# GRU, attention and AUGRU on one core: zeros on TensorE ahead of the first input, another PSUM ring for the item part, results placed by a 0/1 matrix, and another order of the branches

## The chip, the cores and the metric

The kernel runs on one core of one Trainium2 chip. The metric is the device time of one launch in microseconds. The engines are called PE (TensorE matmul; PEld is its weight load), DVE (VectorE), ACT (ScalarE), POOL (GpSimd) and SP (SyncE, which here only issues DMAs). [...]

## The reference

B is 1024 rows, T is 100 steps, every vector has 128 elements. A GRU runs over each row's history; its states are the keys. Each key is scored against the row's item by a small network, the scores are masked and go through a softmax over the steps, and pooled is the weighted sum of the keys. The first 100 elements of pooled are then taken as one attention weight per step for a second recurrence (AUGRU) over the keys. The state at the row's own last step goes with four other features into a three-layer network of sigmoids, which gives one number per row.

```python
def gru_step(h, x_t):
    gi = x_t @ gru_Wih.T + gru_bih
    gh = h @ gru_Whh.T + gru_bhh
    ...
    r = jax.nn.sigmoid(i_r + h_r)
    z = jax.nn.sigmoid(i_z + h_z)
    n = jnp.tanh(i_n + r * h_n)
    h_new = (1.0 - z) * n + z * h
...
feat = jnp.concatenate([keys, q, keys - q, q * keys], axis=-1)
score = _mlp(feat, [(att_W0, att_b0), (att_W1, att_b1), (att_W2, att_b2)], jax.nn.relu)
...
pooled = jnp.einsum('bt,btd->bd', attn, keys)
att_seq = pooled.T[:T]
...
# augru_step, with gates r, u and h_hat like a GRU's
u = a_t[:, None] * u
h_new = (1.0 - u) * h + u * h_hat
...
comb = jnp.concatenate([user_embedding, item_embedding, hist_sum, item_embedding * hist_sum, attention_feature], axis=1)
scores = _mlp(comb, [(ph_W0, ph_b0), (ph_W1, ph_b1), (ph_W2, ph_b2)], jax.nn.sigmoid)
```

## The kernel before, in words

**Tiling.** Vectors lie on the 128 partitions, rows of the batch along the free axis, in two halves of 512 (`HB`, `NH`). All products are fp32[...]. A gate of the GRU is one PSUM bank of 128x512, filled in four strips of 32 partitions (L509)[...]. In the profile's shapes 128*32 stands for the weight tile and 128x512 for the moving operand.

**GRU stage (`gru_phase`).** `Half.gru` (from about L490) does one step of one half: gate r (ACT sigmoid, L521), the recurrent part of gate n (ph), its input part (pi), gate z (pz); then DVE and ACT form u (L529, at t=0 L538), pi+u (L539), tanh (L540), the sigmoid of z (L541), h-n, times z, plus n (L544 to L546), kq = h times item (L548), and `keep` copies the new state to SBUF on ACT (hn, L555). At t=0 there is no recurrent part. PSUM has two rings here: `ps`, six banks with the tag "g" for the gates, and `pa`, two banks with the tag "a", which the attention network uses. `attend(t)` (L673) packs the three layers of the scoring network for steps t, t-1 and t-2 into the tiles pm of ring "a", and `take` (L707 f, L712 mv) reads them. `item_part` multiplies the item by its part of the scoring weights (pq, L245), also in ring "a", and ACT copies the result with the bias to q0 (q, L248). PE does it once, after gru(1) of both halves and just before attend(0). The order on every engine is written out by hand (`manual_schedule`). A tile of a ring can be written again only when its last reader is done.

**Start.** SP issues the loads in this order: wih, the first half of x at t=0 (L191), bih, bhh, the second half (L195), whh, item, then the further x tiles. DVE forms brz, the summed biases of r and z (L201). POOL clears hist (L202) and then the weight tiles that are filled block by block. ACT loads its function table (L205).

**Join.** The rows are sorted by length for the AUGRU, so that a step need only do the rows that are still alive. How many these are at each step depends on the data, so there are three copies of `augru_phase` with different widths, and a number computed on the chip (over_d) chooses: copy 0 if the count of steps over its widths is below 1, copy 1 if it is below 2, else copy 2. The test is a compare-and-branch on every engine at L1281. In the run profiled here copy 0 is taken. Code of the copies lies in the order in which it is written. Copy 0 begins with row gathers by POOL (`load_rows`, L173 and L174: an optional pacing copy and an indirect DMA), PE transposes of the first keys (L1055, copied by ACT, L1056), gates of the first step (`first_step`, L996, L998), ACT's stores of pooled to DRAM (pooled_d), gathers of the sorted attention weights out of it (att_r, L144), and PE products that spread a weight row over the partitions (L1011: first, spare). L1022 multiplies such a row by gate u. L1033 to L1037 transpose the weights and store them as att_d, from where SP loads each step's row (L1042).

**AUGRU stage.** Each step has three gates r, u, h (PE L1073 for the key's part, L1077 for the state's; ACT L1085, L1097, L1098; DVE L1101 to L1114). POOL gathers key rows for later steps in between, at places that `spread` computes. Groups of 128 rows that have come to their end go through `predict(g)`: gather of their features (part, L1148 by `rows_of`), two products (L1163, L1168), sigmoids (L1190), L1196, L1201, L1204, and y (ACT, L1207), one result on each of 128 partitions. `rows_of` then scatters y to the output by POOL's indirect DMA, since sorting has permuted the rows (idx_p holds the places). Groups 1 to 7 are jobs spread over the steps; group 0, the longest rows, is `final`, with last=True, after the last step.

**End.** The program's last line (L1350) holds each engine's closing waits, a drain and a barrier of all engines.

Of the kernel before, what the change touches and what calls it, by code (L numbers as in the profile page):

```python
# [9 lines left out]
F32 = mybir.dt.float32  # L10
# [4 lines left out]
ALU = mybir.AluOpType  # L15
# [4 lines left out]
P = 128  # L20
B = 1024
# [51 lines left out]
FREE_BANK, EARLY_BANKS, LATE_BANKS = 6, (2, 5, 6, 0), (3, 4, 1)  # L73

PR = P // NH


@with_exitstack
def kernel(ctx: ExitStack, tc: tile.TileContext, a: dict, out: bass.AP):
# [38 lines left out]
    pooled_d = dram.tile([B, P], F32, name="pooled_d")  # L118
    rlen_d = dram.tile([NG, P], F32, name="rlen_d")
    part_d = dram.tile([B, M0], F32, name="part_d")  # L120

    def load(name, shape, src=None, dt=F32):
        t = const.tile(shape, dt, name=name)
# [58 lines left out]
    def all_of(steps):  # L182
        for _ in steps:
            pass

    def gru_phase(pools):
# [1 line left out]
        nc.sync.dma_start(out=wih, in_=a["wih"])  # L188
        xp = pools.enter_context(tc.tile_pool(name="xp", bufs=8))
        x_first = xp.tile([P, HB], F32, name="x")  # L190
        nc.sync.dma_start(out=x_first, in_=a["hist_x"][0][:, :HB])  # L191
        bih = load("bih", [P, 3])
        bhh = load("bhh", [P, 3])
        x_second = xp.tile([P, HB], F32, name="x")
        nc.sync.dma_start(out=x_second, in_=a["hist_x"][0][:, HB:])  # L195
        whh = load("whh", [P, 3, P])
        nc.sync.dma_start(out=item, in_=a["item"])
        pre = pools.enter_context(tc.tile_pool(name="pre", bufs=1))

        brz = const.tile([P, 2], F32, name="brz")  # L200
        nc.vector.tensor_add(brz, bih[:, 0:2], bhh[:, 0:2])  # L201
        nc.gpsimd.memset(hist, 0.0)  # L202

        table = pre.tile([P, 1], F32, name="table")
# [18 lines left out]
        ps = pools.enter_context(tc.tile_pool(name="ps", bufs=6, space=PSUM))  # L223
        pa = pools.enter_context(tc.tile_pool(name="pa", bufs=2, space=PSUM))

        def attention_weights():
            w0 = load("w0", [P, 4, A0])
            for i in range(NH):
                for f, s in F0[i]:
                    nc.vector.tensor_add(wk[i][:, f], w0[:, 0, s], w0[:, 2, s])  # L230
                    nc.vector.tensor_copy(wkq[i][:, f], w0[:, 3, s])
                    nc.vector.tensor_sub(wq[i][:, f], w0[:, 1, s], w0[:, 2, s])
                    for f1, s1 in F1[i]:
                        nc.sync.dma_start(out=w12[i][f, f1], in_=a["w1"][s, s1])
                    nc.sync.dma_start(out=bm[i][f, :], in_=a["b0"][s, :])
                sc = slice(SC[i], SC[i] + 1)
                for f1, s1 in F1[i]:
                    nc.sync.dma_start(out=w12[i][f1, sc], in_=a["w2"][s1, :])
                    nc.sync.dma_start(out=bm[i][f1, :], in_=a["b1"][s1, :])
                nc.sync.dma_start(out=bm[i][sc, :], in_=a["b2"].partition_broadcast(1))  # L240

        def item_part():
            for i in range(NH):
                pq = pa.tile([P, HB], F32, tag="a", name="pq")
                nc.tensor.matmul(  # L245
                    pq, lhsT=wq[i], rhs=item[:, ts(i, HB)], start=True, stop=True
                )
                nc.scalar.activation(q0[:, ts(i, HB)], pq, AF.Identity, bias=bm[i])  # L248

        def load_later():  # L250
# [2 lines left out]
            once = dict(tag="once")  # L253
            mask_ti = mid.tile([T, B], I32, name="mask_ti", **once)
            nc.sync.dma_start(out=mask_ti, in_=a["mask_ti"])
            yield

            mask_tb = mid.tile([T, B], BF16, name="mask_tb", **once)
# [201 lines left out]
        class Half:  # L460
# [37 lines left out]
            def gru(self, t, after_gate, after_sum):  # L498

                x = self.x[t]  # L500
                h = self.h[t - 1] if t else hist[:, self.cols]
                hn = hp.tile([P, HB], F32, tag="h", name="hn")
                self.h[t] = hn

                def gate(g, parts):
                    p = ps.tile([P, HB], F32, tag="g", name=f"ps{g}")
                    for j, (w, v) in enumerate(parts):
                        for q in range(P // R):
                            nc.tensor.matmul(  # L509
                                p[ts(q, R), :],  # L510
                                lhsT=w[:, g, ts(q, R)],
                                rhs=v,
                                start=(j == 0),
                                stop=(j == len(parts) - 1),
                            )
# [24 lines left out]
                nc.scalar.activation(pi, pi, AF.Tanh, bias=bih[:, 2:3])  # L540
                nc.scalar.activation(pz, pz, AF.Sigmoid, bias=brz[:, 1:2])  # L541
                after_sum()
                d = wp.tile([P, HB], F32, tag="d", name="d")
                nc.vector.tensor_sub(d, h, pi)  # L544
                nc.vector.tensor_mul(d, pz, d)  # L545
                nc.vector.tensor_add(pi, pi, d)  # L546
                kq = wp.tile([P, HB], F32, name="kq", bufs=2 * NH)
                nc.vector.tensor_mul(kq, pi, item[:, self.cols])  # L548
                self.first[t] = hn, kq
                self.copy = hn, pi  # L550
# [407 lines left out]
    def augru_phase(pools, widths, alive):  # L958
# [41 lines left out]
            return gates  # L1000

        def gather_weights(i):
            r = wp.tile([P, GH, P], F32, name="att_r", bufs=2)
            for g in range(GH):
                gather(r[:, g, :], pooled_d, g, i)
            return r
# [23 lines left out]
        def store_weights(i, p):  # L1030

            for g in range(GH):
                nc.tensor.transpose(p[:, ts(g, P)], sorted_rows[i][:, g, :], ident)  # L1033
            rows_t = wp.tile([P, HB], F32, name="att_t", bufs=2)
            nc.vector.tensor_copy(rows_t, p)
            nc.sync.dma_start(out=att_d[i], in_=rows_t[:T, :])
            load_att(2, i)  # L1037
# [98 lines left out]
        def predict(g, last=False):  # L1136
# [10 lines left out]
            def rows_of(out_ap, in_ap, o, i):  # L1147
                nc.gpsimd.indirect_dma_start(  # L1148
                    out=out_ap,
                    out_offset=o and bass.IndirectOffsetOnAxis(ap=idx_p[:, g : g + 1], axis=0),  # L1150
                    in_=in_ap,
                    in_offset=i and bass.IndirectOffsetOnAxis(ap=idx_p[:, g : g + 1], axis=0),
                )
# [51 lines left out]
            yield  # L1205
            y = sp.tile([P, 1], F32, name="y")
            nc.scalar.activation(y, p2, AF.Sigmoid, bias=later["c2"])  # L1207
            rows_of(out.rearrange("(b o) -> b o", o=1), y, True, None)

        def gathers(q):  # L1210
            for i in range(NH):
# [32 lines left out]
        for t in range(1, T):  # L1244
            if t + 1 in FIRST[2:-1]:
                all_of(ahead)
                ahead, due = gathers(FIRST.index(t + 1) + 1), spread(FIRST.index(t + 1) + 1)
            for i in range(NH):
                half_step(t, i)
                for _ in range(due.pop(0) if due else 0):  # L1250
                    next(ahead, None)

                for n, job in enumerate(list(jobs)):
                    job[0] += 1
                    if n == 0 and job[0] > 2 * G and next(job[1], job) is job:
                        jobs.remove(job)
            left = alive[t + 1] if t + 1 < T else 0
            for g in range(1, HB // PR):
                if left <= g * PR < alive[t]:
                    jobs.append([0, predict(g)])  # L1260
                    if left:
                        next(jobs[-1][1])
            if t == T - G:
                final = predict(0, last=True)
                next(final)
        open_state(T - 1, 1)
        next(final)
        last_state(1)
        for _, job in jobs:
            all_of(job)  # L1270
        all_of(final)

    with ExitStack() as pools, tc.manual_schedule():
# [2 lines left out]
    def augru(n):  # L1276
        with ExitStack() as pools, tc.manual_schedule():
            augru_phase(pools, WIDTHS[n], ALIVE[n])

    over = nc.values_load(over_d, min_val=0, max_val=len(LINES))  # L1280
    with tc.If(over < 1) as fits:  # L1281
        augru(0)
    with fits.Else():
        with tc.If(over < 2) as fits:
            augru(1)
        with fits.Else():
            augru(2)


# [64 lines left out]
```

## Time and profile before

| | us |
|---|---|
| median of 3 runs | 2048.63 |
| the three runs | 2044.19, 2048.96, 2048.63 |
| the profiled execution | 2046.78 |
| its span | 2045.0 |
| PE busy | 1994.6 (98%) |
| DVE busy | 1682.1 (82%) |
| POOL busy | 1260.7 (62%) |
| ACT busy | 944.1 (46%) |

The span is the part of the profiled execution that the profile's page covers, 1.8 us less than its time. A line of groups or of the timeline names the source line, the engine, the operation, what it writes and reads (out<-in), the shapes, and the number of instructions; brackets at the end give the idle time of the engine before it and what ended that. Shown as "busy" are only instructions that compute or move; a q behind an engine's name (POOLq) marks its queue of control and DMA-issuing instructions. The AUGRU begins at about 1403 us on PE; the GRU is all that stands ahead of it.

### The profile page before, as it was taken

What the parts mean: (1) busy time and instruction counts of PE and PEld (TensorE: products, weight loads), DVE (VectorE), ACT (ScalarE), POOL (GpSimd) and SP (SyncE); (2) the same over time, 40 slices, a digit from 0 to 9 for tenths busy, and PEclk for the clock granted to TensorE, in tenths of its full rate; (3) what the DMA queues carried; (4) which work ended last, traced back from release to release, by engine and by line L of the source; (5) the groups of instructions that cost most, each with busy time, mean ns of one, the idle gap of its engine ahead of it and who ended that gap; (6) DMA issues with size and microseconds to landing.
All of it is one profiled execution on the core that took longest, in us unless ns stands there. A gap on an engine that the chain in (4) does not pass through costs nothing.

```text
span 2045.0 us, 41241 instructions
## 1 busy us (share of the span) xinstructions
PE 1994.6 (98%) x15452; PEld 1176.7 (58%) x15452; DVE 1682.1 (82%) x3066; ACT 944.1 (46%) x1708; POOL 1260.7 (62%) x1291
## 2 busy tenths in 40 slices
PE   8999999999999999999999999997699999999997
PEld 3655555555555555555555555544344556679997
DVE  6888989888879887878888888996477777878886
ACT  4444444544544454544454444443244444445554
POOL 0233939579796959595969687997543344443431
PEclk9999999999999999999999999999899999999999
DMA  4553333332234334333433232333332333333322
GB/s 118 101 115 97 98 105 113 98 108 86 89 104 114 118 105 119 113 113 97 141 111 97 91 101 69 96 105 108 122 102 91 91 106 103 95 94 86 95 70 36
DMA packets 241645, 205.66 MB, mean 101 GB/s; under 512 B 59271, under 2 KB 204395, under 8 KB 241435
## 3 DMA queue, kind: packets, MB, share of 16 engines
q1 hardware_dynamic: 227498, 170.43, 29.4%
q0 software_dynamic: 12352, 32.31, 5.6%
q8 instruction: 123, 2.02, 0.4%
q14 instruction: 88, 0.71, 0.1%
q10 hardware_dynamic: 1584, 0.20, 0.1%
HBM read 146.82 MB, written 54.40 MB: 98 GB/s over the span
## 4 chain that ended last, share of the span: by engine, by line
PE 92%; DVE 3%; DMA 2%; issue 1%; ACT 1%; another core or an unknown queue 1%; POOL 0%; SPq 0%; DVEq 0%; ACTq 0%; POOLq 0%
PE ps L509 48%; PE pm L673 16%; PE ph L1077 5%; PE pr L1077 5%; PE pu L1077 4%; PE pu L1073 4%; PE ph L1073 4%; PE pr L1073 4%; DMA rows<-keys_d,idx_k 1%; DVE ps L539 0%; DVE u L529 0%; DVE ps L546 0%; DVE d L545 0%; DVE d L544 0%
## 5 line engine op out<-in xcount | busy, mean ns | idle before, releaser
L509 PE MATMUL ps<-x,wih 128*32 128x512 f32 x4800 | 657.2, 594 | 4.4 <-DMA x<-in_hist_x 4.4
L509 PE MATMUL ps<-hn,whh 128*32 128x512 f32 x4752 | 650.1, 592 | 0.6 <-ACT hn L555 0.6
L509 PEld LDWEIGHTS ps<-x,wih 128*32 128x32 f32 x4800 | 281.7, 110 | 241.7 <-issue 220.4
L509 PEld LDWEIGHTS ps<-hn,whh 128*32 128x32 f32 x4752 | 279.6, 110 | 234.2 <-issue 212.0
L494 POOL TENSOR_TENSOR xm<-x,m 128x512 f32<-128x512 f32 x200 | 234.9, 1174 | 146.0 <-DMA m<-mask_d 145.7
L521 ACT ACTIVATE r<-ps,brz 128x512 f32<-128x512 f32 x200 | 137.7, 688 | 394.9 <-PE ps L509 394.7
L495 POOL TENSOR_TENSOR hist<-hist,xm 128x512 f32<-128x512 f32 x200 | 258.7, 1294 | 15.7
L174 POOL DMA_INDIRECT rows<-keys_d,idx_k x220 | 213.2, 969 | 86.2 <-POOL rows L173 48.5
L610 POOL TENSOR_TENSOR pooled<-pooled,kw 128x512 f32<-128x512 f32 x191 | 245.9, 1287 | 15.0
L609 POOL TENSOR_TENSOR kw<-kt,e 128x512 f32<-128x512 f32 x191 | 206.0, 1078 | 70.6 <-DVE e L782 70.6
L673 PE MATMUL pm<-hn,wk 128*32 128x512 f32 x1200 | 237.7, 592 | 5.0 <-ACT hn L555 2.5
L673 PE MATMUL pm<-kq,wkq 128*32 128x512 f32 x1200 | 237.5, 592 | 0.0
L540 ACT ACTIVATE ps<-ps,bih 128x512 f32<-128x512 f32 x200 | 132.4, 662 | 223.9 <-DVE ps L539 223.9
L1085 ACT ACTIVATE c<-ph,bh 128x96 f32<-128x96 f32 (+41 forms) x198 | 96.5, 488 | 295.9 <-PE ph L1077 240.5
L529 DVE SCALAR_TENSOR_TENSOR u<-ps,bhh,r 128x512 f32<-128x512 f32 x198 | 147.5, 745 | 73.1 <-PE ps L509 69.0
L673 PE MATMUL pm<-mv,w 128*32 128x512 f32 (+1 forms) x808 | 197.6, 592 | 0.5 <-ACT mv L712 0.4
L173 POOL COPY rows<-rest 128x1 f32<-128x1 f32 x188 | 35.3, 188 | 217.5 <-DVE rest L1114 213.5
L544 DVE TENSOR_TENSOR d<-hn,ps 128x512 f32<-128x512 f32 x198 | 136.1, 687 | 35.6 <-ACT ps L540 35.2
L1101 DVE TENSOR_TENSOR pu<-pu,c 128x96 f32<-128x96 f32 (+41 forms) x197 | 88.3, 448 | 87.9 <-ACT c L1085 79.8
L545 DVE TENSOR_TENSOR d<-ps,d 128x512 f32<-128x512 f32 x200 | 138.4, 692 | 25.6 <-ACT ps L541 10.9
L555 ACT COPY hn<-ps 128x512 f32<-128x512 f32 x200 | 116.6, 583 | 92.3 <-DVE kq L548 92.3
L539 DVE TENSOR_TENSOR ps<-ps,u 128x512 f32<-128x512 f32 x200 | 140.0, 700 | 21.5 <-PE ps L509 0.5
(181 smaller groups left out, 3235.3 us busy)
## 6 DMA issues: line engine op xcount, KB each, us to landing
x<-in_hist_x SPq DMA_DIRECT2D x212, 256.0 KB
keys_d<-kt SPq DMA_DIRECT2D x48, 1024.0 KB
m<-mask_d SPq DMA_DIRECT2D x200, 128.0 KB
rows<-keys_d,idx_k POOLq DMA_INDIRECT x220
s_b<-mv SPq DMA_DIRECT2D x200, 8.0 KB
keys_d<-kt SPq DMA_DIRECT2D x32, 64.0 KB
at<-att_d SPq DMA_DIRECT2D x34, 48.0 KB
mask_i<-in_mask SPq DMA_DIRECT2D x8, 200.0 KB
```

The lines of the kernel that those rows point to most:

```text
L174: nc.gpsimd.indirect_dma_start(out=r[:, at, :], out_offset=None, in_=keys_d[q], in_offset=bass.IndirectOffsetOnAxis(ap=idx_k[:, k, i : i + ...
L494: nc.gpsimd.tensor_mul(d, x, m)
L495: nc.gpsimd.tensor_add(acc, acc, d)
L509: nc.tensor.matmul(p[ts(q, R), :], lhsT=w[:, g, ts(q, R)], rhs=v, start=(j == 0), stop=(j == len(parts) - 1),)
L529: nc.vector.scalar_tensor_tensor(out=u, in0=ph, scalar=bhh[:, 2:3], in1=r, op0=ALU.add, op1=ALU.mult,)
L539: nc.vector.tensor_add(pi, pi, u)
L545: nc.vector.tensor_mul(d, pz, d)
L609: eng.tensor_mul(d, k, w)
L610: eng.tensor_add(acc, acc, d)
L673: nc.tensor.matmul(p[i][s, :], lhsT=w[:, s], rhs=v, start=start, stop=stop)
L1073: nc.tensor.matmul(p, lhsT=m[:, 1, :], rhs=k, start=True, stop=False)
L1077: nc.tensor.matmul(p, lhsT=m[:, 0, :], rhs=v, start=False, stop=True)
```

## The change

1. **Start.** ACT issues the loads of x_first and x_second, ahead of its table load; SP keeps the others. A tile idle (128x512) of the ring "kq" is cleared by DVE, and PE multiplies it by itself into two tiles pd of ring "a": eight products of 128*32 by 128x512 whose result nobody reads. brz is formed by DVE behind that memset.
2. **Item part.** pq comes from the gates' ring "g" instead of ring "a".
3. **Results.** Groups 1 to 7 scatter y to early_d, a DRAM tensor that SP clears in the GRU stage. Halfway through the AUGRU (t=50) POOL makes two tiles places (iota, then a comparison with the place of each row of group 0): places[p, c] is 1 where c is row p's place. Behind the last job SP loads all of early_d as all_y, 4 rows of 256, each spread over 32 partitions. For group 0, PE multiplies y, spread over 32 columns, by the four quarters of places into one bank (po), DVE adds all_y, and SP stores the 4x256 results to out. The remaining jobs are run before open_state instead of behind last_state.
4. **Branches.** The test is turned round: copies 1 and 2 stand ahead in the code, copy 0 last.

The diff, without three hunks that only give an old tile its own name as its tag (att_r, att_t, kq):

```diff
@@ -73,6 +73,8 @@
 FREE_BANK, EARLY_BANKS, LATE_BANKS = 6, (2, 5, 6, 0), (3, 4, 1)
 
 PR = P // NH
+BQ = B // (P // R)
+HALF_TIME = T // 2
 
 
 @with_exitstack
@@ -118,6 +120,7 @@
     pooled_d = dram.tile([B, P], F32, name="pooled_d")
     rlen_d = dram.tile([NG, P], F32, name="rlen_d")
     part_d = dram.tile([B, M0], F32, name="part_d")
+    early_d = dram.tile([B, 1], F32, name="early_d")
 
     def load(name, shape, src=None, dt=F32):
         t = const.tile(shape, dt, name=name)
@@ -188,17 +191,16 @@
         nc.sync.dma_start(out=wih, in_=a["wih"])
         xp = pools.enter_context(tc.tile_pool(name="xp", bufs=8))
         x_first = xp.tile([P, HB], F32, name="x")
-        nc.sync.dma_start(out=x_first, in_=a["hist_x"][0][:, :HB])
+        nc.scalar.dma_start(out=x_first, in_=a["hist_x"][0][:, :HB])
         bih = load("bih", [P, 3])
         bhh = load("bhh", [P, 3])
         x_second = xp.tile([P, HB], F32, name="x")
-        nc.sync.dma_start(out=x_second, in_=a["hist_x"][0][:, HB:])
+        nc.scalar.dma_start(out=x_second, in_=a["hist_x"][0][:, HB:])
         whh = load("whh", [P, 3, P])
         nc.sync.dma_start(out=item, in_=a["item"])
         pre = pools.enter_context(tc.tile_pool(name="pre", bufs=1))
 
         brz = const.tile([P, 2], F32, name="brz")
-        nc.vector.tensor_add(brz, bih[:, 0:2], bhh[:, 0:2])
         nc.gpsimd.memset(hist, 0.0)
 
         table = pre.tile([P, 1], F32, name="table")
@@ -222,6 +224,16 @@
         kp = pools.enter_context(tc.tile_pool(name="kp", bufs=3 * NH))
         ps = pools.enter_context(tc.tile_pool(name="ps", bufs=6, space=PSUM))
         pa = pools.enter_context(tc.tile_pool(name="pa", bufs=2, space=PSUM))
+
+        idle = wp.tile([P, HB], F32, tag="kq", name="idle", bufs=2 * NH)
+        nc.vector.memset(idle, 0.0)
+        for _ in range(2):
+            p = pa.tile([P, HB], F32, tag="a", name="pd")
+            for q in range(P // R):
+                nc.tensor.matmul(
+                    p[ts(q, R), :], lhsT=idle[:, ts(q, R)], rhs=idle, start=True, stop=True
+                )
+        nc.vector.tensor_add(brz, bih[:, 0:2], bhh[:, 0:2])
 
         def attention_weights():
             w0 = load("w0", [P, 4, A0])
@@ -241,7 +253,7 @@
 
         def item_part():
             for i in range(NH):
-                pq = pa.tile([P, HB], F32, tag="a", name="pq")
+                pq = ps.tile([P, HB], F32, tag="g", name="pq")
                 nc.tensor.matmul(
                     pq, lhsT=wq[i], rhs=item[:, ts(i, HB)], start=True, stop=True
                 )
@@ -253,6 +265,9 @@
             once = dict(tag="once")
             mask_ti = mid.tile([T, B], I32, name="mask_ti", **once)
             nc.sync.dma_start(out=mask_ti, in_=a["mask_ti"])
+            nc.sync.dma_start(
+                out=early_d.rearrange("(p c) o -> p (c o)", p=P), in_=hist[:, : B // P]
+            )
             yield
 
             mask_tb = mid.tile([T, B], BF16, name="mask_tb", **once)
@@ -1205,7 +1220,49 @@
             yield
             y = sp.tile([P, 1], F32, name="y")
             nc.scalar.activation(y, p2, AF.Sigmoid, bias=later["c2"])
-            rows_of(out.rearrange("(b o) -> b o", o=1), y, True, None)
+            if not last:
+                rows_of(early_d, y, True, None)
+                return
+            p = of_pool("po")[:, :BQ]
+            for q in range(P // R):
+                nc.tensor.matmul(
+                    p[ts(q, R), :],
+                    lhsT=y.to_broadcast([P, R]),
+                    rhs=later["places"][q // 2][:, ts(q % 2, BQ)],
+                    start=True,
+                    stop=True,
+                )
+            all_y = later["all_y"]
+            nc.vector.tensor_add(all_y, p, all_y)
+            nc.sync.dma_start(
+                out=out.rearrange("(q c) -> q c", c=BQ),
+                in_=all_y.rearrange("(q r) c -> q r c", r=R)[:, 0, :],
+            )
+
+        def last_places():
+            own = sp.tile([P, 1], F32, name="own3", bufs=1)
+            nc.gpsimd.tensor_copy(own, idx_p[:, 0:1])
+            later["places"] = []
+            for i in range(NH):
+                row = wp.tile([P, HB], F32, tag="att_r", name="places", bufs=2)
+                nc.gpsimd.iota(
+                    row,
+                    pattern=[[1, HB]],
+                    base=i * HB,
+                    channel_multiplier=0,
+                    allow_small_or_imprecise_dtypes=True,
+                )
+                nc.gpsimd.tensor_scalar(row, row, own, None, ALU.is_equal)
+                later["places"].append(row)
+
+        def earlier_results():
+            later["all_y"] = wp.tile([P, BQ], F32, tag="att_t", name="all_y", bufs=2)
+            nc.sync.dma_start(
+                out=later["all_y"],
+                in_=early_d.rearrange("(q c) o -> q (o c)", c=BQ)
+                .unsqueeze(1)
+                .to_broadcast([P // R, R, BQ]),
+            )
 
         def gathers(q):
             for i in range(NH):
@@ -1263,11 +1320,14 @@
             if t == T - G:
                 final = predict(0, last=True)
                 next(final)
+            if t == HALF_TIME:
+                last_places()
+        for _, job in jobs:
+            all_of(job)
+        earlier_results()
         open_state(T - 1, 1)
         next(final)
         last_state(1)
-        for _, job in jobs:
-            all_of(job)
         all_of(final)
 
     with ExitStack() as pools, tc.manual_schedule():
@@ -1278,13 +1338,13 @@
             augru_phase(pools, WIDTHS[n], ALIVE[n])
 
     over = nc.values_load(over_d, min_val=0, max_val=len(LINES))
-    with tc.If(over < 1) as fits:
-        augru(0)
-    with fits.Else():
+    with tc.If(over > 0) as many:
         with tc.If(over < 2) as fits:
             augru(1)
         with fits.Else():
             augru(2)
+    with many.Else():
+        augru(0)
 
 
 # ---- launch: one core; the host only transposes and reshapes ----
```

More of the change, by code (lines that the diff above doesn't have):

```diff
@@ L546, in gru @@
                 nc.vector.tensor_add(pi, pi, d)
-                kq = wp.tile([P, HB], F32, name="kq", bufs=2 * NH)
+                kq = wp.tile([P, HB], F32, tag="kq", name="kq", bufs=2 * NH)
                 nc.vector.tensor_mul(kq, pi, item[:, self.cols])
@@ L1002, in gather_weights @@
         def gather_weights(i):
-            r = wp.tile([P, GH, P], F32, name="att_r", bufs=2)
+            r = wp.tile([P, GH, P], F32, tag="att_r", name="att_r", bufs=2)
             for g in range(GH):
@@ L1033, in store_weights @@
                 nc.tensor.transpose(p[:, ts(g, P)], sorted_rows[i][:, g, :], ident)
-            rows_t = wp.tile([P, HB], F32, name="att_t", bufs=2)
+            rows_t = wp.tile([P, HB], F32, tag="att_t", name="att_t", bufs=2)
             nc.vector.tensor_copy(rows_t, p)
```

## Prediction

> **What bounds the kernel now.** I read the table of stretches first, then the timeline of the first 34 us, the waits of the stretch where the two halves of the program meet, and last the chain of waits and the end of each engine. Columns of the stretches: start and end, length, then the busy time of PE, PEld, DVE, ACT, POOL, the TensorE clock, the DMA share and GB/s.
>
> ```profile
> 0.00:4.40 4.40, 0.00 (x0) 0.02 (x1) 0.00 (x0) 1.49 (x2) 3.86 (x19) 1.00 0.44 124
> 4.40:20.00 15.60, 14.94 (x120) 4.33 (x124) 10.45 (x27) 5.62 (x9) 1.04 (x6) 1.00 0.45 138
> 20.00:40.00 20.00, 17.54 (x151) 9.10 (x147) 14.88 (x23) 9.55 (x16) 0.00 (x0) 1.00 0.50 114
> 40.00:1380.00 1340.00, 1339.13 (x12478) 729.09 (x12469) 1154.12 (x1753) 634.01 (x1020) 966.20 (x820) 1.00 0.36 104
> 1380.00:1408.00 28.00, 21.74 (x120) 14.28 (x120) 22.74 (x58) 10.99 (x24) 21.90 (x22) 1.00 0.36 106
> 1408.00:1462.00 54.00, 32.88 (x101) 17.79 (x102) 16.86 (x26) 11.71 (x18) 36.59 (x40) 0.78 0.38 107
> 1462.00:2013.00 551.00, 546.22 (x2305) 380.76 (x2304) 446.27 (x1104) 257.44 (x573) 228.17 (x385) 1.00 0.35 94
> 2013.00:2045.00 32.00, 22.18 (x190) 21.32 (x189) 16.80 (x80) 13.27 (x48) 2.96 (x3) 0.91 0.13 21
> ```
>
> PE is 1339 of 1340 us busy in the GRU and 546 of 551 in the AUGRU, and no edit takes work out of those. What the change can touch is the idle rest: 4.4 us at the start, 2.5 between 20 and 40, 27 at the join (1380 to 1462), 10 at the end. The timeline shows the gap at the item part; its last bracket is the idle time before an instruction and what ended it:
>
> ```profile
> 22.81 1.98 PE L245 MATMUL pq<-item,wq 128*128 128x512 f32 x4
> 27.25 0.62 PE L673 MATMUL pm<-hn,wk 128*32 128x512 f32 x2 [2.46 <-ACT q L248]
> ```
>
> At the join two waits end with a releaser that the profile can't place:
>
> ```profile
> DVE spare L1022 <- remote: 11.3, 1, 11.3
> ACT pr L1097 <- remote: 4.2, 1, 4.2
> ```
>
> The end is the last scatter, then the engines' closing instructions. First the last two pieces of the chain, then the branch (L1281) and the drain (L1350), with their first and last start:
>
> ```profile
> 2025.62 11.44 issue
> 2037.30 0.99 POOL out L1148
> ```
>
> ```profile
> L1281 PEldq COMPARE_BRANCH  x2: 92/2189/4286, 1403.0 to 2036.3; - x2
> L1281 POOLq COMPARE_BRANCH  x2: 41/43/45, 1414.3 to 2037.1; - x2
> ```
>
> ```profile
> L1350 POOLq DRAIN  x3: 40/107/4063, 2040.1 to 2044.7; - x3
> ```
>
> At the first branch (1403.0 on PE, 1414.3 on POOL) every engine falls through, for about 0.1 us or less. At the second the engines jump over two unused copies of the AUGRU: PE's takes 4.29 us, and POOL, which jumps at 2037.1 with the scatter issued, comes to its drain at 2040.1. That drain lasts 4.06 us, and the program ends behind it at 2045.0: 8.0 us after y is ready (2036.76 + 0.26 = 2037.02).
>
> [...] weight loads come 0.86 us apart from 4.38, 0.43 apart from 8.54, 4.0 us after the first matmul. [...]
>
> **The change, part by part**, against the profiled execution, 2046.78 (span 2045.0 and 1.8 around it).
>
> *1. Start.* ACT now issues the two x loads. An issue takes 0.42 us (the x row at 1.19 on SP), so x_first is issued at about 0.75 instead of 1.19 and lands at 3.9 to 4.1 instead of 4.38. ACT's table load moves 0.85 later; its first use is at 6.41: nothing. SP's bih, bhh, whh and item come 0.4 to 1.0 earlier: nothing to lose. The zero tile is 128x512 on DVE, 0.7 us like the DVE rows of that shape, so PE begins at about 1.3 (0.75 to 1.4). The 8 zero products are 16 passes through the array (fp32 takes two, 56 records for 28 products at the start); a group of four passes is 0.86 at half clock, so they last 3.4 us and end near 4.75, after x is in: real work begins 0.3 to 0.4 later than before. If the clock rises before it, all real work is at full rate. [...] What counts is the chain pi, DVE L539, tanh, three DVE steps, hn, because PE stands 0.64 us at 13.23 for hn. Gate pi is ready at 8.1 now; [...] So the gain is between 1.2 and −0.5; the middle is 0.4. brz moves behind the memset, and needs bhh (5.50 now), so nothing. **−0.4.** The zeros use both buffers of the ring "a", whose next user is attend(0) at 27 us, on PE itself: no wait.
>
> *2. Item part.* In the ring "a" attend(0) must wait until ACT has read pq (q, 26.51 to 27.78): 2.46 us of PE. In the gates' ring attend no longer waits, but the pq tiles take two of the six gate buffers, so they wait for earlier gates' readers themselves, and gru(2) finds two buffers fewer. Its pi of half 0 gets the buffer of pi(1) of half 1, free only after ACT's hn copy (33.80 to 34.38 now). attend and pr could start about 1.1 us earlier, but pi was reached at 33.29 before, and the chain behind hn(1) of half 1 doesn't move up by itself, since DVE and ACT form it (DVE is busy 14.9 of 20 us). Mostly the same stall shifted by one step. Bounds: −1.1 (all kept) and +0.3. **0.0.**
>
> *3. Branch order.* The common copy now stands last, so every engine jumps at the entry instead of at the end. Price per engine from the end of before: PE 4.3, DVE 2.9, ACT 3.1, POOL 3.0, SP 3.9, from branch to next instruction. At the entry: PE jumps at 1403.0 and can go on at 1407.3, where it now does transposes for k (1403.81 on); ACT, at 1406.6, has to arrive too, so the two overlap; DVE, done at 1415.8, is idle until 1429.7; SP, at 1418.7, waits until 1437.4; POOL jumps at 1414.3 while the DMA queue still works on its row gathers until about 1421. The covers are thus the row gathers and then the attention-weight gathers that wait for the pooled stores: PE waits for those until 1428.78. What isn't covered are ACT's three pooled stores (1416.35 to 1417.9), which come 0.4 to 1.6 later behind ACT's later steps and gate those gathers; they land around 1421, as POOL gets there at 1421.7. About 0.3, with 1.5 as the upper bound where nothing else goes wrong; below nothing not, unless the burst at the join changes (rival B). **+0.3.**
>
> *4. POOL's 0/1 matrix.* Two iotas and two compares of 128x512 and a tiny copy at t=50: no such row exists in before; POOL's 128x512 rows take 1.08 to 1.29 (L609, L610), so some 5 us, in a stage where POOL is 228 of 551 us busy, behind which row gathers queue that are issued steps ahead. **0**; bound +1 if a gather came late.
>
> *5. Other stores.* SP clears early_d with one small store behind mask_ti; seven scatters go to early_d instead of out: as before. SP loads all_y once the last early scatter has landed (2025.6), some 2.3 us later, done at 2028: hidden by the 9 us to y.
>
> *6. End.* From y at 2037.02: 0.06 to PE; four products of 32x256, 8 passes of half the width, 0.75 to 1.0 with the way to PSUM (four passes of 100*80 plus transfer take 0.74 from 2035.18 to ACT's start); DVE add 128x256, between the rows 128x96 (0.25) and 128x512 (0.70), 0.45; SP's store to DRAM. The nearest rows for that are att_d (issue at 1437.41, its reader issued at 1440.01: 2.6) and the first pooled store (2.3). Then SP's ten closing waits, of 0.06 each, and the barrier: 0.3 to 0.7 and 0.8. Sum 5.2 against 8.0. POOL has then nothing after 2026, and its drain (4.06) is hidden, and no engine jumps. Bounds −2.3 to −3.2, **−2.8**; 0 if the drain stays last.
>
> Sum: −0.4 + 0 + 0.3 + 0 − 2.8 = −2.9. That is 2043.9 against the profiled execution and 2045.7 against the median 2048.63, as the profiled one lies 1.85 under it. I take the middle, 2044.8.
>
> **Rivals.** *A, the entry jump is exposed; slower.* Place: 1403 to 1430. [...] idle PE falls back to half clock (it did at 1408 to 1411)[...] Price 6.0 instead of 0.3, total +2.8: 2049.6 against the profiled run, 2051.4 against the median. For it: all of PE's idle at the join hangs on gathers, ACT is in that chain. Against it: the gathers on POOL's queue run to 1421 whatever PE does. It decides once over 3.2 us of the jump reach the path. *B, the unplaced waits move; faster.* At 1437 to 1459 signals arrive late (11.3 and 4.2 us) and the profile doesn't say why. [...] another place of the code changes it: up to −11 more, about 2034. For it: two waits with no releaser, in a burst. Against it: the burst stays. *C, nothing of the end is won.* If POOL's drain or another closing step still takes 4 us after the last store, part 6 is 0 and the sum −0.1: 2046.7 to 2048.5. For it: the drain is the last step in before. Against it: POOL has been idle for 11 us by then.
>
> **How the numbers follow.** Forecast 0.61, with its own range 2041.5 to 2048 (start ±0.8, item −1.1 to +0.3, end ±0.5, and runs that lie ±2.4 about their middle); A 0.14; B 0.12; C 0.13. The range for 8 in 10 leaves out B and the far part of A: 2040 to 2050.5. This kernel's measurement can tell about 0.3%, 6.1 us: faster than 2042.5 holds B and a tenth of the forecast, 0.17; slower than 2054.8 only the far half of A, 0.07; the rest, 0.76, is within.
>
> **What would show it.** Right: clock up and pi ready before 8 us; no 2.46 wait at attend, but one of an L509 gate for ACT hn soon after; PE's first step behind the entry branch 4.3 us late and "first" within 1 us of its distance; the end within 5.5 us of y with the store, not the drain, last. Wrong: "first" 3 us or more later in the join, the 11.3 us wait gone or doubled, a gate of gru(2) waiting longer than 3 us, or a drain of 4 us behind the last store.

## The result, and the profile after

The changed kernel takes 2042.5 us (median of 9 runs, 2040.21 to 2044.79), the kernel before 2048.26 (9 runs, 2044.19 to 2050.77). The ratio is 0.9974, with a 95% interval of 0.9966 to 0.9982: 5.3 us faster, between 3.7 and 7.0 (the plain medians lie 5.8 apart). The forecast was 2.9 us faster, so the direction was right and the size too small by nearly a half. The profiled execution shown here took 2044.42 us (span 2042.5), 1.9 above its median, where that of before lay under its own; so the two profiles are 2.4 us apart, not 5.3, and the stages have to be compared one by one.

The stretches of the changed kernel, cut as those of before but without the first, in which the zeros now keep PE busy for 2.95 us (start and end, length, busy time of PE, PEld, DVE, ACT, POOL, clock, DMA share, GB/s):

```profile
4.40:20.00 15.60, 14.25 (x124) 3.82 (x120) 10.44 (x27) 5.54 (x9) 1.02 (x6) 1.00 0.43 126
20.00:40.00 20.00, 20.00 (x176) 6.06 (x172) 17.46 (x27) 11.58 (x19) 0.00 (x0) 1.00 0.49 115
40.00:1380.00 1340.00, 1336.78 (x12452) 567.36 (x12444) 1152.66 (x1751) 631.56 (x1018) 967.21 (x822) 1.00 0.36 104
1380.00:1408.00 28.00, 20.86 (x112) 13.37 (x113) 22.94 (x59) 9.54 (x21) 22.10 (x21) 0.96 0.42 125
1408.00:1462.00 54.00, 32.14 (x102) 18.34 (x103) 14.69 (x23) 12.76 (x20) 34.97 (x38) 0.70 0.38 99
1462.00:2013.00 551.00, 546.59 (x2306) 381.11 (x2305) 446.18 (x1102) 257.04 (x572) 232.53 (x390) 1.00 0.36 94
2013.00:2042.50 29.50, 23.90 (x203) 22.09 (x202) 17.76 (x83) 13.87 (x51) 1.97 (x2) 0.91 0.16 25
```

Between 20 and 40 us PE has no idle time left: 20.00 busy, where it was 17.54. Between 40 and 1380 it is busy 2.4 us less than before; where, follows below. The PE timeline at the item part, where the bracket of 2.46 us stood:

```profile
24.74 0.62 PE L688 MATMUL pm<-hn,wk 128*32 128x512 f32 x2
28.20 1.04 PE L524 MATMUL ps<-x,wih 128*32 128x512 f32 x8
```

attend(0) follows pq at once, and gru(2) begins at 28.20 instead of 30.71. That the gain stays is seen on ACT. First the kernel before, then the changed one; r is the gate of gru(2), hn the state of step 1, half 1:

```profile
33.21 0.69 ACT L521 ACTIVATE r<-ps,brz 128x512 f32<-128x512 f32 x1 [5.43 <-PE ps L509]
33.80 0.58 ACT L555 COPY hn<-ps 128x512 f32<-128x512 f32 x1
```

```profile
30.16 0.69 ACT L536 ACTIVATE r<-ps,brz 128x512 f32<-128x512 f32 x1 [2.37 <-PE ps L524]
30.75 0.58 ACT L570 COPY hn<-ps 128x512 f32<-128x512 f32 x1
```

DVE had long finished the state that this copy takes; its last step on it, in the kernel before, is:

```profile
28.30 0.69 DVE L548 TENSOR_TENSOR kq<-ps,item 128x512 f32<-128x512 f32 x1
```

That ends at 28.99, and the copy began 4.8 us later, because it stood behind r in ACT's queue, and ACT had been idle 5.43 us waiting for the r of gru(2). When PE comes to gru(2) earlier, r comes, and hn with it: 3.05 us earlier.

The waits of the changed kernel whose releaser the profile can't place:

```profile
DVE spare L1037 <- remote: 15.5, 1, 15.5
DVE ps L554 <- remote: 3.5, 1, 3.5
```

The first stands at the join, where before had 11.3 and 4.2. The second is new, at 119 to 123 us. It accounts for only part of the 2.4 us by which PE is less busy after 40 us: 0.7 us of them lie between 40 and 130, and 1.1 behind 1370, where PE is done with the scoring products 1.4 us earlier than before.

The entry branch (duration min/median/max in ns, first and last start):

```profile
L1341 PEldq COMPARE_BRANCH  x1: 6858/6858/6858, 1401.0 to 1401.0; - x1
```

And the end, on the timeline:

```profile
2037.58 0.26 ACT L1222 ACTIVATE y<-p,c 128x1 f32<-128x1 f32 x1 [0.47 <-PE p L1219]
2037.98 1.08 PE L1228 MATMUL po<-places,y 128*32 128x256 f32 x8 [0.44 <-ACT y L1222]
2039.12 0.42 DVE L1236 TENSOR_TENSOR all_y<-po,all_y 128x256 f32<-128x256 f32 x1 [4.02 <-PE po L1228]
2039.57 0.57 SPq L1237 DMA_DIRECT2D out<-all_y  x1
```

```profile
L1410 POOLq DRAIN  x3: 40/113/6714, 2022.3 to 2042.2; - x3
```

The end comes 4.6 us behind y (2037.84 to 2042.45) instead of 8.0. POOL's long drain, 6.7 us now, begins at 2022.3 and is over at 2029.0, before y. But y itself comes 0.8 us later than before. At the last scoring product 1.4 us of what the item part gave were left; the join then took 1.0 us longer, and the AUGRU 1.25.

### The profile page after: what moved, and what is told of

It reads as the page before. It is cut to its first block, busy times and chain, and to the rows that moved or that the text cites. A ratio compares the mean times of both kernels' runs of the same rounds, so it can differ in the third digit from the quotient of the medians.

```text
span 2042.5 us, 41284 instructions
## 1 busy us (share of the span) xinstructions
PE 1997.5 (98%) x15476; PEld 1012.9 (50%) x15476; DVE 1682.6 (82%) x3068; ACT 943.4 (46%) x1708; POOL 1263.7 (62%) x1295
## 4 chain that ended last, share of the span: by engine, by line
PE 91%; DVE 3%; POOL 2%; issue 1%; DMA 1%; ACT 1%; another core or an unknown queue 1%; DVEq 0%; POOLq 0%; SPq 0%; ACTq 0%
PE ps L524 47%; PE pm L688 16%; PE ph L1092 5%; PE pr L1092 4%; PE pu L1092 4%; PE ph L1088 4%; PE pr L1088 4%; PE pu L1088 4%; POOL pooled L625 1%; POOL kw L624 1%; DMA rows<-keys_d,idx_k 1%; DVE pu L1116 0%; DVE ps L554 0%; PE p L1183 0%
## 5 line engine op out<-in xcount | busy, mean ns | idle before, releaser
L524 PE MATMUL ps<-x,wih 128*32 128x512 f32 x4800 | 617.2, 593 | 0.0
L524 PE MATMUL ps<-hn,whh 128*32 128x512 f32 x4752 | 611.2, 592 | 1.4 <-ACT hn L570 1.4
L524 PEld LDWEIGHTS ps<-x,wih 128*32 128x32 f32 x4800 | 218.5, 110 | 300.0 <-issue 297.1
L524 PEld LDWEIGHTS ps<-hn,whh 128*32 128x32 f32 x4752 | 216.6, 110 | 296.4 <-issue 292.5
L688 PE MATMUL pm<-hn,wk 128*32 128x512 f32 x1200 | 222.2, 592 | 2.2 <-ACT hn L570 2.2
L688 PE MATMUL pm<-kq,wkq 128*32 128x512 f32 x1200 | 222.1, 592 | 0.0
L559 DVE TENSOR_TENSOR d<-hn,ps 128x512 f32<-128x512 f32 x198 | 136.0, 687 | 35.9 <-ACT ps L555 35.5
L554 DVE TENSOR_TENSOR ps<-ps,u 128x512 f32<-128x512 f32 x200 | 140.0, 700 | 24.9 <-remote 3.5
L560 DVE TENSOR_TENSOR d<-ps,d 128x512 f32<-128x512 f32 x200 | 138.3, 692 | 26.0 <-ACT ps L556 11.3
```

What stands on the lines that cost most here:

```text
L524: nc.tensor.matmul(p[ts(q, R), :], lhsT=w[:, g, ts(q, R)], rhs=v, start=(j == 0), stop=(j == len(parts) - 1),)
L688: nc.tensor.matmul(p[i][s, :], lhsT=w[:, s], rhs=v, start=start, stop=stop)
```

## The experiments

In two of the five series of runs (that of the result, and the one with the three kernels e_order, b_clear and e_clear) the kernel before took 2044 to 2048 us, in the other three 2019 to 2020; the record names a different chip for each of the four series after that of the result, so the kind may be that of the chip. The stretch from the first product with the attention weights to the first AUGRU step (read at DVE's first h of a step, L1105 before and L1120 after) takes 29 to 34.5 us in the former and 12.5 to 14.5 in the latter, whatever the kernel; the long waits at the join with an unplaced releaser (8 to 18 us) are there in the former only. Each ratio is to the kernel before in the same series, and stages are compared within one kind. Each run has one profile. The last scoring product is PE's last into pm. Kernels are called by their labels: e_ is the changed kernel with an edit, b_ the kernel before with one.

**The changed kernel again (again).**

> The changed kernel once more, for a second profile. If the item part and the end carry the gain, the profile again shows gru(2) begin at 28.2 us (30.7 before), y about 1 us off that of before, and the end 4.7 us behind y (8.0 before); ratio to before near 0.9974. If the gain were luck of the join (the waits with an unplaced releaser), those parts would stay and the time would fall back to within 2 us of before.

Measured: ratio 0.9988 (0.9980 to 0.9996), 2015.92 against 2018.78. gru(2) began at 28.24, the end 4.18 behind y, but only 2.4 us of the gain was there. So the item part and the end do carry over, and about half of the first gain does not: neither theory as stated. The profile again had the new wait (DVE, L554, 4.1 us; the late signal, below), though none at the join.

**pq back in the ring of attend (e_pq_a).**

> The changed kernel with pq back in the ring of attend. Theory (ACT's hn copy stood behind the r of gru(2), so the whole chain moves up with PE): 3.0 us slower than the changed kernel, the 2.5 us wait of attend for q is back. Rival (my prediction: the wait only moves, nothing is kept): no difference, 0 to 0.3 us.

```diff
-                pq = ps.tile([P, HB], F32, tag="g", name="pq")
+                pq = pa.tile([P, HB], F32, tag="a", name="pq")
```

Measured: 1.0004 (0.9996 to 1.0013), 3.4 us above the changed kernel in the same series. That is the theory, and nothing of my rival. In its profile the price is even higher: behind the wait of 2.46 us PE's groups of products (four tiles of 128*32 side by side, in the 0.43 us that one pass of a 128*128 tile takes at L1073 in before) come 0.85 us apart from 27.8 to 31.1 us instead of 0.43, so PE ran at half rate there (granted clock 0.91 between 20 and 40 us, 1.00 in the run again), and hn of step 1, half 1, came 4.7 us later than in the run again. The two profiles of the kernel before and that of b_clear have the same wait and kept the full rate. How often PE falls to half rate there is not known; the next run gives the cleaner price.

**The item part alone, in the kernel before (b_item).**

> The kernel before with pq in the gates' ring and nothing else. Theory: 3.0 us faster than before, gru(2) 2.5 us earlier and the rest from hn(1). Rival (prediction): no gain, within 0.3 us.

Its edit is the same line the other way. Measured: 0.9985 (0.9978 to 0.9991), 3.0 us faster with an interval of 1.8 to 4.4. One line gives as much as the whole change did in that kind of series (2.4, interval 0.8 to 4.0).

**The common copy first again (e_first).**

> The changed kernel with the common copy first in the code again, as before. Theory: the entry jump costs 2.5 us at the join, through ACT's three late pooled stores; taken away, the first product with the weights comes 2.5 us earlier, and the engines jump at the end again (SP 3.9 us, beside the landing of the store and on the path of the barrier: +2). Together within 1 us of the changed kernel. Rival (jump hidden at the join, as predicted, 0.3): about 2 us slower than the changed kernel.

The edit puts the last lines of the program back as they were before. Measured: 0.9990 (0.9982 to 0.9998), 0.9 above the changed kernel. The end took 6.75 us behind y (4.18 in the run again), and from the last scoring product to DVE's first use of the weights passed 35.25 us. Over all profiles that distance is 34.6 where the common copy stands first (33.9 to 35.25, five profiles) and 36.5 where it stands last (35.9 to 37.1, six profiles with ACT's stores in their old place): the entry jump costs 1.9 there. Given back at the end, it leaves the two orders nearly even, as the theory had it.

**The last results by POOL's scatter (e_scatter).**

> The changed kernel with POOL's scatter of the last results as before; order of branches as changed. Theory: no jump stands before POOL's drain, but the scatter does: y to end 6.2 us (0.28 to the scatter, 1.0 issue, drain 4.1, barrier 0.8), 1.5 us slower than the changed kernel. Rival (the drain of 4 us came of the jump): drain gone, y to end about 4.3, nothing lost.

The edit takes part 3 of the change out. Measured: the end 6.13 us behind y, as reckoned; its scatter:

```profile
2007.53 0.99 POOL L1160 DMA_INDIRECT out<-y,idx_p  x1 [12.93 <-ACT y L1219]
```

POOL's drain stands in the trace from 0.04 us behind y, ahead of the scatter, and ends 4.0 us behind the scatter's end. But the time was 0.9987 (0.9980 to 0.9993), no worse than with part 3 in, though the end is 1.95 us longer. The profile gives the likely reason: this kernel had no late signal at 117 to 128 us. Of the ten profiles of the result, of this series and of the next, the six with SP's clear of early_d have one, the four without it none.

**The kernel before again (before_again).**

> The kernel before once more, for a second profile on the same chip as the others. It shows whether the join takes 30 us from the last scoring product to the first product with the weights, the end 8.0 us behind y, and whether the late signals at 117 to 124 us and at 1437 to 1459 us come in this kernel too or belong to the change.

Measured: one run, 2017.42 us, 2.0 below the median of the other runs of that kernel there. From the last scoring product to the first product 29.5 us, the end 8.04 behind y, no late signal anywhere. So the one at 117 to 128 us belongs to the change, and those at the join to the series.

**No zeros (e_nozero).**

> The changed kernel without the zero tile and its eight products; ACT still loads x. Theory (the zeros end 0.7 us after x is in and the clock rises at most 1.8 us earlier, so the two cancel): the first hn copy within 0.4 us of the changed kernel's 12.6, the time within 1 us. Rival (they warm the clock for a real gain, 0.4 to 1.2 as in my prediction): hn 0.4 to 1.2 later and the time with it.

The edit takes out the tile idle and the eight products. Measured: 0.9988 (0.9982 to 0.9995), the same ratio as with them in the run again; hn at 12.41. In nine kernels with zeros hn began at 11.70 to 12.65 (mean 12.27), in five without at 12.20 to 12.59 (mean 12.40). The weight loads of the changed kernel show both halves of the trade:

```profile
4.15 0.15 PEld L524 LDWEIGHTS ps<-x,wih 128*32 128x32 f32 x4 [0.80 <-DMA x<-in_hist_x]
4.87 0.20 PEld L524 LDWEIGHTS ps<-x,wih 128*32 128x32 f32 x4 [0.56 <-issue]
5.72 0.20 PEld L524 LDWEIGHTS ps<-x,wih 128*32 128x32 f32 x4 [0.66 <-issue]
6.57 0.12 PEld L524 LDWEIGHTS ps<-x,wih 128*32 128x32 f32 x4 [0.65 <-issue]
7.00 0.12 PEld L524 LDWEIGHTS ps<-x,wih 128*32 128x32 f32 x4 [0.31 <-issue]
```

x is in at 4.15, but the first product with it begins at 4.87, behind the zeros; the loads go from 0.85 to 0.43 us apart at 6.6, in before at 8.5. This step is what is called the rise of the clock here and in the forecast; the granted clock of the profile is 1.00 on both sides of it. Without zeros the loads begin at 4.11 and are still 0.85 apart at 8.38. When the clock rises differs from run to run: in the nine profiles with zeros between 4.8 and 7.4 us, and only in the three in which it had risen by 5.4 did hn come at 11.70 to 11.85. On average what is gained and what is lost nearly balance.

**All stores of pooled by SP (e_spst).**

> The changed kernel with all eight stores of pooled issued by SP ahead of its branch, none by ACT. Theory (the entry jump costs because ACT's three stores come late behind PE's stall, and the weight gathers wait for them): the stretch from the last scoring product to the first product with the weights falls from 32.4 to 33.9 by about 1.8 us towards 30.8, the time too. Rival [...]: stretch and time unchanged within 0.5.

```diff
-        for to, t in later["att", 1] + later["att", 0][G - 1 :]:
+        for to, t in later["att", 1] + later["att", 0]:
...
-        for to, t in later["att", 0][: G - 1]:
-            nc.scalar.dma_start(out=to, in_=t)
```

Measured: 0.9983 (0.9977 to 0.9990), but the stretch 32.75 us, not shorter. The last store was issued only 0.7 us earlier relative to the last scoring product (24.4 against 25.1 in the run again): eight stores on one queue took 4.7 us, longer than five and three on two (3.3 and 1.5 in the run again). The remedy was a poor one and says little on the cause.

**ACT's stores earlier (e_order).**

> The changed kernel with ACT's three stores of pooled ahead of the gates of half 1 and the second pair of k copies instead of behind them; nothing else. Theory (the jump costs because those stores land late): they end 2 to 2.7 us earlier, the weight gathers begin 1.5 to 2 earlier, and the stretch from the last scoring product to the first product with the weights falls from 32.4 by 1 to 2 us. Rival (PE's own backlog behind its 6.8 us jump binds just as much): the gathers come earlier, the first product does not, time within 0.5 us of the changed kernel or later, as ACT's copies for PE come 1.5 later.

```diff
-        gates = [first_step(i) for i in range(NH)]
-        for i in range(NH):
-            load_key(1, i, (FREE_BANK, None)[i])
+        gates = [first_step(0)]
         for to, t in later["att", 0][: G - 1]:
             nc.scalar.dma_start(out=to, in_=t)
+        gates.append(first_step(1))
+        for i in range(NH):
+            load_key(1, i, (FREE_BANK, None)[i])
```

Measured: 0.9980 (0.9972 to 0.9988). The changed kernel itself was not in that series; e_clear was, and lies 1.7 us above. The last store was issued at 22.8 us behind the last scoring product (25.1 to 26.5 with the order as changed) and the first gather at 27.7 (28.6 to 29.75), but the first product at 33.2, no earlier, and DVE's first use at 36.6. The lines of this kernel:

```profile
1421.52 0.95 POOL L147 DMA_INDIRECT att_r<-pooled_d,idx  x1 [2.42 <-DMA pooled_d<-s_b]
1426.99 0.93 PE L1026 MATMUL first<-ident,att_r 128*128 128x128 f32 x6 [0.72 <-issue]
1429.53 0.79 PE L1026 MATMUL first<-ident,att_r 128*128 128x128 f32 x2 [1.61 <-DMA att_r<-pooled_d,idx]
```

PE comes to the first product 5.5 us after the first gather is issued, having worked off what its jump had held up, and then does six of the eight at once; in the kernel before it began with two of them and waited for gathers in between. So in this profile PE's backlog binds at the first product and a gather still at the last, and the theory of the stores falls as the sole cause. How the 1.9 us divide between stores and backlog stays open: in the last run below (best), with the same order, DVE's first use came at 35.6 us, ahead of all six profiles with the stores in their old place.

**The clear alone, in the kernel before (b_clear).**

> The kernel before with nothing added but SP's clear of early_d at 28 us. Theory: the late signal of 2.6 to 4.1 us at 117 to 125 us appears, 2 us slower than before. Rival: as before, within 0.5 us.

The edit adds early_d and its clear and nothing else; nobody reads it. Measured: 1.0015 (1.0008 to 1.0021), 3.1 us slower with an interval of 1.6 to 4.3. The late signal is there, and SP's stop; the waits, then SP's timeline:

```profile
ACT ps L545 <- remote: 3.1, 1, 3.1
```

```profile
119.74 0.41 SPq L482 DMA_DIRECT2D x<-in_hist_x  x1
120.20 6.06 SPq L487 DMA_DIRECT2D m<-mask_d  x1
```

In the profile the state of step 11 comes 1.9 us later than in the kernel before, though the first state came 0.4 us earlier. A store of 4 KB at 28 us, which nobody waits for, costs about what the new end wins over the scatter (1.95), or more.

**The clear on ACT (e_clear).**

> The changed kernel with early_d cleared by ACT at the start (behind its table load) instead of by SP at 28 us, so that SP's queue holds the same DMAs as before in the GRU. In all six kernels with SP's clear SP stands 5.6 to 6.8 us in the issue of m at 117 to 123 us, and a signal of PE arrives 2.6 to 4.1 us late; in the four without it SP stands 3.9 to 4.2 us one DMA later, in the store of keys, and no signal is late. Theory (the extra DMA moves SP's stop by one place): the late signal is gone, the time 2 us below the changed kernel. Rival (the late signals come with the zeros or the earlier phase of the GRU): unchanged.

The edit moves the clear behind ACT's table load. Measured: 0.9989 (0.9982 to 0.9996). The late signal was still there (3.8 us), and SP stopped for 7.2 us at the same m. SP's queue now holds two DMAs fewer than before's, so its count is not what decides: the theory falls in that form. What is left is that one DMA more is issued ahead, on either queue.

**Both repairs (best).**

> The changed kernel with the order of ACT's stores of the run before (behind the first gates of half 0) and early_d cleared in the AUGRU (step 8, by SP, from a small zero tile) instead of in the GRU. Theory (any DMA more ahead of 117 us brings the late signal there, whichever queue it is on, and costs 2 to 3 us): no late signal at 117 to 125 us, SP's long stop one DMA later in the store of keys, and 2 to 3 us below the run with the order alone, so a ratio to before of 0.9965 to 0.9972. Rival (the stop has another cause, such as the clear itself or the phase of the start): the late signal is still there, ratio 0.998.

The edit is that of the stores above, and the clear moved to step 8 of the AUGRU, from a small zero tile. Measured: 0.9974 (0.9965 to 0.9984), 2014.87 against 2019.87: 5.0 us faster in a kind of series in which the changed kernel had been 2.4 faster. Its SP timeline:

```profile
115.98 0.43 SPq L497 DMA_DIRECT2D m<-mask_d  x1
120.67 5.00 SPq L596 DMA_DIRECT2D keys_d<-kt  x2
125.76 2.87 SPq L354 DMA_DIRECT2D over_d<-over_i  x1
```

No late signal, and the state of step 8, half 1, is done at 127.9 us (130.4 in the run again, of which 0.9 is the earlier start of this run). By ratio this is the fastest version in that kind of series; the changed kernel's was 0.9988 there, in another series, and the two intervals overlap. The changed kernel's 0.9974 in the result belongs to the other kind and can't be set beside it.

## Why the prediction was right in direction and small in size

The range held, and the sign came out as forecast, but by errors that partly cancelled, so that the sum came so near is in part luck. By its own steps:

1. *Start, −0.4.* About −0.1 (hn 12.27 against 12.40 on average), and no difference in time. The bounds held, though the two times of the clock's rise behind them were assumed and not shown by a trace of before: by profile hn came from 0.7 earlier to 0.25 later, as the clock rose early or late. The middle was not: I took the clock's gain and the later start of real work for less than fully balanced. (By the lines of the forecast itself the clock of before rose 4.1 us behind the first product, not 4.0.)
2. *Item part, 0.0.* **This step failed.** It measured −3.0 (b_item), −3.4 (e_pq_a the other way). I reasoned that hn of half 1 is formed by DVE and ACT and doesn't move with PE. But ahead of that copy in ACT's queue stood r of gru(2), for which ACT sat idle 5.43 us: r began at 33.21 and the copy at 33.80, though its operand was done at 28.99. The line was on the timeline I had read. The bound of −1.1 was too tight for the same reason.
3. *Branch order, +0.3.* Mis-sized, in two terms: PE's jump took 6.56 to 6.86 us at the entry, not the 4.3 of the end; and ACT's stores, forecast 0.4 to 1.6 later, came 3.4 later on average (the last is issued by 25.1 to 26.5 us behind the last scoring product, by 21.8 to 22.7 with the common copy first). From the last scoring product to the first AUGRU step pass 44.2 us on average with the common copy first (before_again, b_item, e_first; 43.8 to 44.8) and 46.2 with it last (again, e_pq_a, e_scatter, e_nozero; 45.5 to 46.9): +2.0. Rival A, in which PE's jump pushes the transposes, the first gates and with them the gathers, had the place and the engine, but its price of 6.0 was too high as mine was too low. What it set for the half clock was assumed; by profile PE's granted clock was 0.50 from 1408 to 1411 in the kernel before, and from 1406 to 1416 in the changed one. My sign for it, "first" 3 us or more later, did come in the result's profile (33.9 us behind the last scoring product instead of 30.1), but the path goes through the last gather, and DVE's first use came only 2.6 later.
4. *0/1 matrix, 0.* Nothing in the traces speaks against it: the AUGRU, from its first step to y, took 569.8 us with it (again) and 569.7 without (e_scatter). It was not tried alone.
5. *Other stores, "as before".* **This step failed too**: SP's clear cost 3.1 by the times of b_clear (1.6 to 4.3), and 2.2 and 1.8 by the profiles (from the first hn to the last scoring product: b_clear against before, again against e_scatter). I priced the DMA's data and issue, and put at nothing what one more DMA early in the kernel can do to the later ones; how it does it is open.
6. *End, −2.8.* −3.4 to −3.9: from 8.0 us behind y to 4.6 or 4.2 (po takes 1.1 or 0.6). The mechanism was right, the drain hidden and no jump. Part 3 and part 4 need each other: with the scatter 6.1, with the jump 6.75.

With 1.9 for the clear, within what the profiles show, the sum for the series of 2019 to 2020 is −0.1 − 3.0 + 2.0 + 1.9 − 3.6 = −2.8, measured −2.4 (0.8 to 4.0 faster); with the 3.1 of b_clear it would be −1.6. In the series of 2044 to 2048, the result's among them, the stretch from the last scoring product to the first AUGRU step was no longer with the jump (65.6 and 61.9 in the changed kernel and e_clear) than without (64.6 and 62.5 in before and b_clear): the late signals there seem to cover the 2.0. That gives −0.1 − 3.0 + 0 + 1.9 − 3.4 = −4.6, measured −5.3 (3.7 to 7.0). The AUGRU itself was then some 1.3 longer (577.2 and 576.3 without the change, 578.5, 577.7 and 578.3 with it), which would make it −3.3; these are single profiles, and the 0.7 to 2.0 that remain (1.2 more with the 3.1 of b_clear) are not placed. Of rival B, that much is seen: the unplaced waits shift by a few microseconds, and by far not by its 11. Rival C did not come.

Two causes stay open. Why one DMA more, on SP or on ACT, brings SP's stop from the store of keys to a load of m and a signal of PE 2.6 to 4.1 us late, is not known; that it does is shown by nine profiles with an early clear, five without one, and b_clear's time. And why signals are late at the join in some series only was not tried: spreading the burst of row gathers would have been the run for it.

## What to carry to other kernels

When a wait is removed, don't ask which engine forms the next operand, but what stands ahead of it in that engine's queue: here a copy behind an instruction that waited for PE moved up 3.05 us when PE came 2.51 earlier. A small DMA that nobody waits for need not be free: here one of 4 KB cost 3.1 us (1.6 to 4.3). Run it alone before it goes in with a gain. The jump over the unused copies was paid at one end or the other: PE had 3.6 to 4.3 us at the end or 6.56 to 6.86 at the entry, the other engines 2.9 to 3.9 at the end of before, from branch to next instruction. Put it where the engine that pays longest has slack behind it.

## What the runs showed of the hardware that was not expected

A taken branch cost PE 3.6 to 4.3 us at the end and 6.56 to 6.86 at the entry. POOL's closing drain is on record with 4.06 us in the kernel before, 5.2 in e_scatter and 6.7 in the changed kernel, but in the latter two its record begins ahead of POOL's last indirect DMA. Counted from the end of that DMA, or from the drain's own start where that is later, it lasted 4.0 to 4.8 us in all fourteen profiles, 4.06 even where the scatter had ended 1.8 us before. In the changed kernel POOL's last DMA ended at 2024.8, 13 us ahead of y, and the drain was over before y; in the kernel before it ended 1.3 us behind y (2038.29), and the drain was the last step ahead of the barrier. After the wait of 2.46 us at attend PE fell to half rate in one profile (e_pq_a, 0.85 us between groups) and in three others did not (0.43). The kernel before spends 14.5 or 34.5 us in the same stretch of the join, by series.
